# A second attention layer whose fp32 products become three single-pass products of parts, with shared arrays for the parts

## The chip, the cores and the metric

The kernel runs on one core of a Trainium2 chip. The metric is the device time of one execution in microseconds (us). The times of the kernel before are 3044.53, 3044.64 and 3044.72 us; the median is 3044.64.

The engines have short names in the profile: PE is TensorE (matmuls; PEld is its weight load), DVE is VectorE, ACT is ScalarE, POOL is GpSimd and SP is SyncE, which here issues most of the DMAs. Each engine runs its own instructions in program order; between engines there are semaphores.

## What is computed

The input is x with 2 batches, 128 channels and 64 x 64 positions, which are L = 4096 tokens per batch. Two layers follow each other:

```python
# layer 0: group norm, 4 heads of attention with rotary positions, projection, residual
x = _L0_conv_ref(x, ...)
# layer 1, on tokens t [2, 4096, 128]
t = _to_tokens(x)
t = t + _L1_attn_ref(_ln_t(t))
t = t + _L1_ffn_ref(_ln_t(t), sigma, phi, M_u, M_phi_plus, M_phi_minus, log_weights, gumbel)
x = _from_tokens(t, x)

def _L1_attn_ref(x):                       # the "second attention"
    scores = jnp.einsum('bsd,btd->bst', x, x)
    attn_weights = jax.nn.softmax(scores, axis=-1)
    return jnp.einsum('bst,btd->bsd', attn_weights, x)
```

`_ln_t` normalises each token over its 128 channels. `_L1_ffn_ref` is a spectral mixing: a causal convolution of the normalised tokens with 16 filters, then for each filter a product with a 128 x 128 matrix (`Mpp` for the plain sequence, `Mpm` for the sequence with alternating signs), and a short autoregressive part with 3 taps. The four branches on shortened sequences are weighted by a one-hot choice.

The second attention has one operand in three places: queries, keys and values are all the normalised tokens y. The scores are therefore a symmetric matrix.

## The kernel before: how the work is tiled and ordered

**Stages.** Layer 0 (`layer0`) runs attention pair by pair; beside its last pieces it is handed a generator, `beside_last()`, which normalises batch 0 for the second attention. Then `attend(0, ...)` and `attend(1, ...)` do the second attention, and a loop over convolution chunks (`chunk`, `convolve`, `mix`, `back`) does the spectral mixing.

**Second attention, L860 to L958.** The 4096 tokens are 8 blocks of 512 (NQ = 8) or 32 tiles of 128 (NT = 32). Because the scores are symmetric, only steps (j, i) with i >= j are computed, 36 per batch. A step computes the 512 x 512 block of scores as four tiles of 128 x 512 (`scores`, matmul on L877), takes exp on ACT with a fixed shift and a running sum into `den` (L886), and keeps the result as `e`, in two buffers. `turn` (L890) transposes it for steps with i > j: four transposes of 128 x 128 into one PSUM bank (L893), then a copy by ACT to SBUF that also sums (L895). `weigh` (L900) multiplies tiles of y with four tiles of `e`, or of the turned `eT`, and adds in the PSUM tile `oacc`, which has one bank for block j (summed over the whole row of steps) and one for block i (added to `oT` by DVE in each step, L930 or L932). `close` (L904) ends a row j: `fin` (L907 or L909), the reciprocal sums `rden` (L911, L912), four transposes (L915) and four updates of the tokens `tok` (L918).

The order is written out by hand in the loop at the end of `attend`: a step's scores are issued between the transposes of the step before (`late`), then the sums of the step before, and `next(beside, None)` steps a chain of side work five times in a full step. A generator that yields does one small piece each time. For batch 0 the chain is `chain(left, steps, filters, matrices)`: what layer 0 left, the normalising of batch 1 (L721 to L742), the filter tables, and the mixing's matrices. For batch 1 it is `chain(feed, second_parts)`: the convolution's input of batch 0 (`feed`, L960 to L1030) and the low parts of the matrices (L1043 to L1049).

**Matrices, L828 to L857.** For each of 16 filters, `Mpp` and `Mpm` of four branches are loaded into the tile `raw`, which has one buffer (L847, L848); DVE makes the weighted sum `pm` of four branches (`weighted_sum`, L704 once and L706 three times), writes sum and difference back into `raw` (L853, L854), casts them to the rounded type in `mx` (L855), subtracts to get the low part (L856), and SP stores this to DRAM (L857).

**Types.** A matmul of fp32 operands (F32) shows two records per product in the trace. A matmul of operands in the rounded type F32R is one pass with one record. Before, batch 1's scores, as well as the mixing (`mix`, L1166), are already written as three F32R products of a high part (the value rounded) and a low part (value minus high part). Batch 0's scores and all sums of both batches are F32.

**Statistics.** `LayerStats` (L667 to L700) takes bn_stats and bn_aggr for each of 32 token tiles on DVE (`take`), then a reciprocal root (`close`), then `normed` (L697) writes normalised tiles.

Of the kernel before, what the change touches and what calls it, by code (L numbers as in the profile page):

```python
# [44 lines left out]
WC = 4  # L45
# [18 lines left out]
def conv_attn_hybrid(ctx: ExitStack, tc: tile.TileContext, io):  # L64
# [36 lines left out]

    def group_norm(b, bank, p1, px):
# [3 lines left out]
        xn = px.tile([P, L], F32, tag="b", name=f"xn{b}")  # L106
# [57 lines left out]
    def layer0(tok, px, last, side, beside_last):  # L164


        with ExitStack() as l0:
# [222 lines left out]
            for n, (b, pr) in enumerate(units):  # L390
                if n + 1 < len(units):
                    nxt = units[n + 1]
                    if nxt[1] == 0:
                        norm = group_norm(nxt[0], bank, p1, px)
                        xn = next(norm)
                        after = prepare(*nxt, xn)
                        beside = chain(beside, norm, after[3])
                    else:
                        after = prepare(*nxt, xn)
                        beside = chain(beside, after[3])  # L400
                else:
                    beside = beside_last()
# [39 lines left out]
    def layer0_any(tok, px, last, side, beside_last):  # L442

        with ExitStack() as l0:
# [212 lines left out]
            for _ in beside_last():  # L657
                pass
# [53 lines left out]
    def layers(st, layer0):  # L712
        psum_a, right0, right1, right2 = (st.enter_context(ExitStack()) for _ in range(4))

        tok = [None, pool(right0, "tok1", side="right").tile([P, NI, C], F32, name="tok1")]
        tok[0] = pool(right1, "tok0", side="right").tile([P, NI, C], F32, name="tok0")
        last = pool(right2, "last", 2, side="right")
        px = pool(right2, "px", side="right")
        side = [None]

        def normalise(b, p, ytag, yttag):  # L721


            y = p.tile([P, NT, C], F32, tag=ytag, name=f"y{b}")
            yT = p.tile([P, L], F32R if b else F32, tag=yttag, name=f"yT{b}")

            def steps():
                stats = LayerStats(p, tok[b], f"a{b}")
                yield from stats.steps()
                for i in range(NQ):  # L730
                    for t in range(4 * i, 4 * i + 4):
                        stats.normed(y[:, t, :], t)
                    yield
                    pt = side[0](f"yT{b}_{i}")
                    for t in range(4):
                        nc.tensor.transpose(pt[:, bass.ts(t, P)], y[:, 4 * i + t, :], ident)
                    nc.vector.tensor_copy(yT[:, bass.ts(i, 512)], pt)
                    if b:
                        low = p.tile([P, 512], F32, tag="fin", name=f"low{i}")
                        nc.vector.tensor_tensor(low, pt, yT[:, bass.ts(i, 512)], ALU.subtract)  # L740
                        nc.sync.dma_start(lows_y[i], low)
                    yield  # L742

            return y, yT, steps()

        ys = [None, None]

        def beside_last():
            *ys[0], steps = normalise(0, px, "a", "b")
            yield from steps  # L750
# [8 lines left out]
        mxr = ffw.tile([P, NK, 2, C], F32R, name="mx")  # L759
        lows_y = dram.tile([NQ, P, 512], F32, name="lows_y")  # L760
        lows_m = dram.tile([NK, P, 2, C], F32, name="lows_m")
# [10 lines left out]
        pi = pool(st, "ff_in", 4)  # L772
# [55 lines left out]
        def matrices(p):  # L828
# [16 lines left out]
            for k in range(NK):  # L845
                raw = p.tile([P, NBR, 2, C], F32, tag="raw", name=f"raw{k}")
                nc.sync.dma_start(raw[:, :, 0, :], io["mpp"][:, k].rearrange("i d e -> d i e"))  # L847
                nc.sync.dma_start(raw[:, :, 1, :], io["mpm"][:, k].rearrange("i d e -> d i e"))  # L848
                yield
                pm = p.tile([P, 2, C], F32, tag="pm", name=f"pm{k}")  # L850
                weighted_sum(pm, raw, coef[:, k, :])
                own = raw[:, 0]
                nc.vector.tensor_tensor(own[:, 0, :], pm[:, 0, :], pm[:, 1, :], ALU.add)  # L853
                nc.vector.tensor_tensor(own[:, 1, :], pm[:, 0, :], pm[:, 1, :], ALU.subtract)  # L854
                nc.vector.tensor_copy(mxr[:, k], own)  # L855
                nc.vector.tensor_tensor(own, own, mxr[:, k], ALU.subtract)  # L856
                nc.sync.dma_start(lows_m[k], own)  # L857
                yield

        def attend(b, p, y, yT, oT, beside, closed=lambda j: None, lo=None):  # L860
# [6 lines left out]
            products = [(yT, yT)]  # L867
            if lo is not None:
                low = lo()
                products = [(low, yT), (yT, low), (yT, yT)]  # L870

            def scores(j, i, e, h):
                ps = psum.tile([P, 2, 512], F32, tag="st", name=f"y{b}_{j}_{i}_{h}")
                for q in range(2):
                    t = 4 * j + 2 * h + q
                    for n, (a, c) in enumerate(products):
                        nc.tensor.matmul(  # L877
                            ps[:, q, :],
                            a[:, bass.ts(t, P)],
                            c[:, bass.ts(i, 512)],  # L880
                            start=(n == 0),
                            stop=(n == len(products) - 1),
                        )
# [6 lines left out]
            def turn(j, i, e, u):  # L890
# [3 lines left out]
                eT = p.tile([P, 512], F32, tag="eT", name=f"eT{b}_{j}_{i}_{u}", bufs=5)  # L894
                nc.scalar.activation(eT, pt, AF.Copy, accum_out=den[:, 4 * i + u, j : j + 1])  # L895
                return eT

            def weigh(acc, first, es, start, stop):
                for t, e in enumerate(es):
                    nc.tensor.matmul(  # L900
                        acc, y[:, first + t, :], e, start=(start and t == 0), stop=(stop and t == len(es) - 1)
                    )
# [20 lines left out]
            def sums(j, i, e, eT, acc):  # L923
                es = [e[:, t, :] for t in range(4)]
# [15 lines left out]
            for j in range(NQ):  # L940
                acc = psum.tile([P, 2, 512], F32, tag="acc", name=f"oacc{b}_{j}", bufs=1)
                for i in range(j, NQ):
                    e = p.tile([P, 4, 512], F32, tag="e", name=f"ey{b}_{j}_{i}", bufs=2)
                    eT = []
                    for h in range(2):
# [86 lines left out]
        with ExitStack() as l1:  # L1032
            p1 = pool(l1, "l1")
            *ys[1], steps = normalise(1, p1, "y", "yT")
            fw = transform(p1)
            with ExitStack() as part:
                p = pool(part, "l1_a")
                oT = ffw.tile([P, NQ, 512], F32, tag="lo", name="oT0")
                attend(0, p1, *ys[0], oT, chain(left, steps, filters(p, fw), matrices(p)))
            right2.close()  # L1040
            mxl = ffw.tile([P, NK, 2, C], F32R, tag="lo", name="mxl")

            def second_parts():  # L1043
                for k in range(0, NK, 2):
                    low = p.tile([P, 2, 2, C], F32, tag="low", name=f"low_m{k}", bufs=1)
                    nc.sync.dma_start(low, lows_m[k : k + 2].rearrange("k p s c -> p k s c"))
                    yield
                    nc.vector.tensor_copy(mxl[:, k : k + 2], low)
                    yield  # L1049

            with ExitStack() as part:
# [3 lines left out]
                def closed(j):  # L1055
                    fed.take(range(4 * j, 4 * j + 4))
                    fed.close(range(4 * j, 4 * j + 4))

                oT = p.tile([P, NQ, 512], F32, name="oT1", bufs=1)

                def lo():
                    lo = p.tile([P, L], F32R, name="lo", bufs=1)
                    for i in range(NQ):
                        own = (p1, "fin") if i % 2 == 0 else (p, "low")
                        low = own[0].tile([P, 512], F32, tag=own[1], name=f"low_y{i}", bufs=1)
                        nc.sync.dma_start(low, lows_y[i])
                        nc.vector.tensor_copy(lo[:, bass.ts(i, 512)], low)
                    return lo

                attend(1, p1, *ys[1], oT, chain(feed(0, p, bank, fw), second_parts()), closed, lo)  # L1070
        right1.close()
# [4 lines left out]
        px = pool(st, "ff_x")  # L1076
        late_pool = pool(right1, "late", 2, side="right")

# [9 lines left out]
        def chunk(b, ro, ch, s):  # L1088
# [4 lines left out]
            for n in range(2):  # L1093
                u = f"{b}_{ro}_{ch}_{s}_{n}"
                tt = pi.tile([P, WC // 2, 2 * BP * NK], F32, tag="tt", name=f"tt{u}")
                ut = pi.tile([P, WC // 2, C], F32, tag="ut", name=f"ut{u}")
# [24 lines left out]
        xl = px.tile([P, NK * 512], F32R, name="xl", bufs=1)  # L1121
# [58 lines left out]
        def back(b, ro, oh, outs, p):  # L1180
# [7 lines left out]
            if ro == 0:  # L1188
                outs[b] = p.tile([P, L], F32, tag="out", name=f"out{b}", bufs=1)
            outr = outs[b].rearrange("p (j q r) -> p r q j", q=BP, r=2)  # L1190

            def turned(p4):
# [5 lines left out]
                v = (px if end else p).tile(  # L1198
# [41 lines left out]
        for b in range(B):  # L1240
            for ro in range(2):
                oh = (late_pool if ro else px).tile([P, L], F32, tag="oh", name=f"oh{b}_{ro}", bufs=1)
                for ch in range(NCH):
                    acc = pc.tile([P, 512], F32, tag="acc", name=f"m{b}_{ro}_{ch}")
                    for s in range(2):
                        u = f"{b}_{ro}_{ch}_{s}"
                        halves = chunk(b, ro, ch, s)
                        xh = px.tile([P, NK, WC * 4 * 2 * BP], F32R, tag="xh", name=f"xh{u}", bufs=2)
# [7 lines left out]
                if (b, ro) == (0, 0):  # L1256
                    right1.close()
                    right0.close()
                    late_pool = pool(right0, "out", 2, side="right")
# [132 lines left out]
```

## Time and profile before

| quantity | value |
|---|---|
| median of three runs | 3044.64 us |
| profiled execution | 3042.84 us |
| its span in the trace | 3041.0 us (1.84 us lie around it) |
| granted TensorE clock, mean | 0.995 |
| PE busy | 2968.3 us (98%) |
| DVE busy | 1322.6 us (43%) |
| ACT busy | 1833.4 us (60%) |
| POOL busy | 656.3 us (22%) |
| first score of batch 0, of batch 1 | 1031.56, 1452.38 us |
| first convolution matmul | 1883.2 us |

The page has six parts: busy time by engine, the span in 40 slices, the DMA queues, the chain of work that ended last, the costliest groups of instructions, and the DMA issues. In a group's row, `out<-in` are the tiles written and read, then count, busy sum in us, mean ns of one, and after the second bar the idle time of that engine just before these instructions, with who released it. Matmul records overlap, so the mean of a record is longer than the distance from one to the next. The view by windows gives the busy time of each engine in a stretch; the chain view follows the last work back to what released it.

### The profile page before, as it was taken

The page shows a single profiled execution, that of the slowest core. Times are in us where ns is not written, and L with a number is a line of the kernel's source. Part 1 is how long each engine was busy: PE and PEld are TensorE (multiplying, and loading weights), DVE is VectorE, ACT ScalarE, POOL GpSimd, SP SyncE. Part 2 cuts the span into 40 slices and gives each one's busy share as a digit, 9 for nine tenths or more (in the row PEclk, how much of TensorE's full clock was granted, in tenths as well). Part 3 has the DMA queues.
Part 4 walks back from the last instruction along what each step waited for, and adds up shares of the span by engine and source line. Part 5 has one row for each costly group of instructions (what it writes and reads, how often), then busy time and mean ns, then how long its engine had stood idle before and what let it go on. Part 6 is the DMA issues. An engine that isn't in the chain of part 4 may idle for free.

```text
span 3041.0 us, 36995 instructions
## 1 busy us (share of the span) xinstructions
PE 2968.3 (98%) x13216; PEld 1696.2 (56%) x13216; DVE 1322.6 (43%) x2236; ACT 1833.4 (60%) x2363; POOL 656.3 (22%) x1328
## 2 busy tenths in 40 slices
PE   5999999999999999999999999999999999999997
PEld 3555555555455554444555554656666666666665
DVE  5363662364332243321311113555555555555553
ACT  4999999999999734344343444444444444444442
POOL 4031120031100010000101001444444444444440
PEclk9999999999999999999999999999999999999999
DMA  4021220020000003200211000333333334333331
GB/s 145 25 82 46 63 58 6 25 81 20 6 4 6 16 25 114 70 28 4 70 35 35 10 1 16 95 88 94 92 84 80 85 73 114 80 88 81 79 81 49
DMA packets 163583, 171.52 MB, mean 56 GB/s; under 512 B 45136, under 2 KB 109408, under 8 KB 163392
## 3 DMA queue, kind: packets, MB, share of 16 engines
q1 hardware_dynamic: 119584, 131.80, 15.1%
q0 software_dynamic: 40816, 34.04, 5.1%
q10 hardware_dynamic: 2992, 3.22, 0.3%
q8 instruction: 110, 1.80, 0.3%
q14 instruction: 81, 0.66, 0.1%
HBM read 128.58 MB, written 23.40 MB: 50 GB/s over the span
## 4 chain that ended last, share of the span: by engine, by line
PE 62%; DMA 2%; DVE 2%; issue 0%; ACT 0%; SPq 0%; DVEq 0%; ACTq 0%
PE m L1166 25%; PE oacc L900 13%; PE cv L1134 9%; PE y L877 6%; PE eT L893 3%; PE ar L977 1%; PE pf L994 1%; PE bk L1216 1%; DMA raw<-in_mpm 1%; PE vt L1207 0%; DMA lows_m<-raw 0%; DVE pm L706 0%; PE o L915 0%; DMA low_y<-lows_y 0%; PE tT L972 0%; DMA low_m<-lows_m 0%
## 5 line engine op out<-in xcount | busy, mean ns | idle before, releaser
L421 ACT ACTIVATE e<-s 128x1536 f16<-128x1536 f32 (+1 forms) x704 | 936.7, 1430 | 36.4 <-PE s L178 31.5
L1143 ACT CAST xh<-cv 128x1024 fp32r<-128x1024 f32 x512 | 494.7, 1019 | 525.6 <-PE cv L1134 524.7
L1144 DVE TENSOR_TENSOR xl<-cv,xh 128x1024 fp32r<-128x1024 f32 x512 | 603.3, 1220 | 436.8 <-ACT xh L1143 346.9
L1109 POOL DMA_DIRECT2D ut<-rows x1024 | 488.4, 485 | 689.8 <-PE cv L1134 579.9
L178 PE MATMUL s<-qs,ks 128*128 128x512 f16 x2048 | 557.6, 379 | 8.5 <-ACT e L421 3.4
L178 PE MATMUL acc<-e,v 128*97 128x512 f16 x2048 | 557.3, 379 | 3.4 <-DVE accs L377 0.2
L886 ACT ACTIVATE ey<-y,nshift 128x512 f32<-128x512 f32 x288 | 195.7, 687 | 428.5 <-PE y L877 426.0
L1166 PE MATMUL m<-xh,mxl 128*128 128x512 f32 x1024 | 411.3, 402 | 0.0
L1166 PE MATMUL m<-xh,mx 128*128 128x512 f32 x1024 | 404.8, 395 | 0.0
L178 PEld LDWEIGHTS <-v 128*97 128x97 bf16 x2048 | 254.6, 124 | 214.8 <-issue 12.9
L178 PEld LDWEIGHTS <-ks 128*128 128x128 f16 x2048 | 200.6, 99 | 227.5 <-issue 42.5
L1134 PE MATMUL cv<-tt,ut 32*128 32x512 f32 x2048 | 299.4, 644 | 2.1 <-DVE xl L1144 2.1
L1166 PE MATMUL m<-xl,mx 128*128 128x512 f32 x1024 | 290.9, 416 | 0.8 <-DVE xl L1144 0.5
L1166 PEld LDWEIGHTS m<-xl,mx 128*128 128x128 f32 x1024 | 178.6, 189 | 175.0 <-issue 104.7
L900 PE MATMUL oacc<-ey,y 128*128 128x512 f32 x576 | 262.8, 592 | 0.0
L1166 PEld LDWEIGHTS m<-xh,mxl 128*128 128x128 f32 x1024 | 192.4, 188 | 91.1 <-issue 47.8
L1166 PEld LDWEIGHTS m<-xh,mx 128*128 128x128 f32 x1024 | 192.6, 188 | 43.6
L900 PE MATMUL oacc<-eT,y 128*128 128x512 f32 x448 | 206.7, 604 | 3.7 <-DVE oT L930 3.4
L877 PE MATMUL y<-yT 128*128 128x512 f32 x432 | 198.5, 531 | 1.7 <-ACT ey L886 1.7
L377 DVE COPY accs<-acc 97x512 f32<-97x512 f32 x64 | 44.2, 691 | 282.5 <-PE acc L178 282.4
L900 PEld LDWEIGHTS oacc<-ey,y 128*128 128x128 f32 x576 | 103.6, 190 | 99.3 <-issue 98.5
L900 PEld LDWEIGHTS oacc<-eT,y 128*128 128x128 f32 x448 | 80.9, 189 | 115.9 <-issue 81.6
(177 smaller groups left out, 2257.2 us busy)
## 6 DMA issues: line engine op xcount, KB each, us to landing
tt<-tables SPq DMA_DIRECT2D x1024, 64.0 KB, 3.3
tab<-in_rot SPq DMA_DIRECT2D x32, 512.0 KB, 4.2
ut<-rows POOLq DMA_DIRECT2D x1024, 16.0 KB, 3.2
qs<-term POOLq DMA_DIRECT2D x128, 64.0 KB, 2.2
rows<-uh SPq DMA_DIRECT2D x64, 128.0 KB, 1.9
ks<-term POOLq DMA_DIRECT2D x96, 64.0 KB, 1.9
accs<-back SPq DMA_DIRECT2D x32, 128.0 KB, 2.3
raw<-in_mpp SPq DMA_DIRECT2D x16, 256.0 KB, 3.0
```

The costliest lines, as they stand in the source:

```text
L178: tc.keep_in_program_order(nc.tensor.matmul(*args, **kw))
L377: nc.vector.tensor_copy(accs[:, bass.ts(half, 512)], acc[: NV * CH + 1, :])
L421: nc.scalar.activation(e[:, own, :], ps[:, own, :], AF.Exp, scale=SCORE_SCALE)
L877: nc.tensor.matmul(ps[:, q, :], a[:, bass.ts(t, P)], c[:, bass.ts(i, 512)], start=(n == 0), stop=(n == len(products) - 1),)
L886: nc.scalar.activation(e[:, 2 * h + q, :], ps[:, q, :], AF.Exp, bias=nshift, accum_out=den[:, t, i : i + 1])
L893: nc.tensor.transpose(pt[:, bass.ts(t, P)], e[:, t, bass.ts(u, P)], ident)
L900: nc.tensor.matmul(acc, y[:, first + t, :], e, start=(start and t == 0), stop=(stop and t == len(es) - 1))
L1109: nc.gpsimd.dma_start(ut[part, :, :], rows[b][ci, row : row + BP, w0 : w0 + WC // 2, :])
L1134: nc.tensor.matmul(pu[:, h, :], ut[grp, w % 2, :], tt[grp, w % 2, :], start=True, stop=True)
L1143: nc.scalar.copy(hi, pu.rearrange("d h (c k) -> d k h c", k=NK))
L1144: nc.vector.tensor_tensor(seconds[n % 2][:, :, w, 64 * g2 : 64 * g2 + 64].rearrange("d k (h c) -> d k h c", h=2), pu.rearrange("d h (c k) ...
L1166: nc.tensor.matmul(acc, m, x, start=(s == 0 and w == 0 and i == 0), stop=(s == 1 and w == WC - 1 and i == len(products) - 1),)
```

## The change

**Products.** All scores and all sums of both batches become three F32R products. The tokens' parts are `hi`, `lo` (token-major, for the sums) and `hiT`, `loT` (channel-major, for the scores). `e` is split on DVE into `ep0` (a cast) and `ep1` (e minus ep0), four tiles each per step, in `sums`. `eT` is split in `turn`: ACT copies the bank to `eT0`, DVE subtracts that from the same bank to get `eT1`.

**Arrays.** `hi`, `lo`, `hiT`, `loT` exist once. Batch 0's parts are made beside layer 0; the low parts go to DRAM (`lows`) and come back at the start of `attend(0, ...)`, a block ahead of the first row's steps (`ready`). Batch 1's parts overwrite them block by block while batch 0 is still running: `normalise` waits at `gate`, which `closed(j)` opens after row j. For that the chain of batch 0 becomes `left, filters, matrices, steps`. In batch 1, `closed(j)` loads two of the mixing's matrices and writes their high and low parts over the blocks of `hiT` and `loT` that are no longer needed; `mxr` and `mxl` are views of these two arrays. `matrices` now stores full sums to DRAM and neither casts nor subtracts.

**Convolution.** The tables and tokens of a chunk lie in two halves of fixed arrays (`tables_in` in the place of `hi`, `tokens_in`), taken in turn, where four rotating buffers were. Pools are rearranged accordingly, and some outputs take the place of `tok`.

The core of the diff:

```diff
-        def normalise(b, p, ytag, yttag):
...
+        def normalise(b, p, stage, gate=None):
+
+            stats = LayerStats(p, tok[b], f"a{b}")
+            yield from stats.steps()
+            for i in range(NQ):
+                while gate is not None and gate[0] <= i:
                     yield
+                cols = bass.ts(i, 512)
+                y = stage(i, 0)
+                for t in range(4):
+                    stats.normed(y[:, bass.ts(t, P)], 4 * i + t)
+                nc.vector.tensor_copy(hi[0][:, cols], y)
+                yield
+                pt = side[0](f"yT{b}_{i}")
+                for t in range(4):
+                    nc.tensor.transpose(pt[:, bass.ts(t, P)], y[:, bass.ts(t, P)], ident)
+                nc.vector.tensor_copy(hiT[0][:, cols], pt)
+                low = (stage(i, 1), stage(i, 0)) if b == 0 else (loT[0][:, cols], lo[0][:, cols])
+                for n, (src, first) in enumerate(((pt, hiT[0][:, cols]), (y, hi[0][:, cols]))):
+                    nc.vector.tensor_tensor(low[n], src, first, ALU.subtract)
+                    if b == 0:
+                        nc.sync.dma_start(lows[i, n], low[n])
+                yield
...
                 nc.vector.tensor_tensor(own[:, 1, :], pm[:, 0, :], pm[:, 1, :], ALU.subtract)
-                nc.vector.tensor_copy(mxr[:, k], own)
-                nc.vector.tensor_tensor(own, own, mxr[:, k], ALU.subtract)
-                nc.sync.dma_start(lows_m[k], own)
+                nc.sync.dma_start(mx[k], own)
                 yield
...
-                    for n, (a, c) in enumerate(products):
+                    for n, (a, c) in enumerate(((hiT, hiT), (hiT, loT), (loT, hiT))):
...
-                eT = p.tile([P, 512], F32, tag="eT", name=f"eT{b}_{j}_{i}_{u}", bufs=5)
-                nc.scalar.activation(eT, pt, AF.Copy, accum_out=den[:, 4 * i + u, j : j + 1])
+                eT = [p.tile([P, 512], F32R, tag=f"eT{n}", name=f"eT{n}_{b}_{j}_{i}_{u}", bufs=5) for n in range(2)]
+                nc.scalar.activation(eT[0], pt, AF.Copy, accum_out=den[:, 4 * i + u, j : j + 1])
+                nc.vector.tensor_tensor(eT[1], pt, eT[0], ALU.subtract)
...
-                for t, e in enumerate(es):
-                    nc.tensor.matmul(
-                        acc, y[:, first + t, :], e, start=(start and t == 0), stop=(stop and t == len(es) - 1)
-                    )
+                for t, (e, rest) in enumerate(es):
+                    own = bass.ts(first + t, P)
+                    for n, (a, c) in enumerate(((hi, e), (lo, e), (hi, rest))):
+                        nc.tensor.matmul(
+                            acc,
+                            a[0][:, own],
+                            c,
+                            start=(start and t == 0 and n == 0),
+                            stop=(stop and t == len(es) - 1 and n == 2),
+                        )
...
-                es = [e[:, t, :] for t in range(4)]
+                es = []
+                for t in range(4):
+                    es.append([p.tile([P, 512], F32R, tag=f"ep{n}", name=f"ep{n}_{b}_{j}_{i}_{t}", bufs=4) for n in range(2)])
+                    nc.vector.tensor_copy(es[t][0], e[:, t, :])
+                    nc.vector.tensor_tensor(es[t][1], e[:, t, :], es[t][0], ALU.subtract)
...
-                attend(0, p1, *ys[0], oT, chain(left, steps, filters(p, fw), matrices(p)))
...
+                gate = [0]
+
+                def ready(i):
+                    for n in range(2) if i == 0 else [i + 1]:
+                        if n < NQ:
+                            low = p.tile([P, 2, 512], F32, tag="low", name=f"low{n}")
+                            nc.sync.dma_start(low, lows[n].rearrange("n p c -> p n c"))
+                            nc.vector.tensor_copy(loT[0][:, bass.ts(n, 512)], low[:, 0])
+                            nc.vector.tensor_copy(lo[0][:, bass.ts(n, 512)], low[:, 1])
+
+                def closed(j):
+                    gate[0] = j + 1
...
+                steps = normalise(1, p1, stage, gate)
+                attend(0, p1, chain(left, filters(p, fw), matrices(p), steps), closed, ready)
...
                 def closed(j):
                     fed.take(range(4 * j, 4 * j + 4))
                     fed.close(range(4 * j, 4 * j + 4))
+                    own = slice(2 * j, 2 * j + 2)
+                    m = p.tile([P, 2, 2, C], F32, tag="m", name=f"m{j}")
+                    nc.sync.dma_start(m, mx[own].rearrange("k p s c -> p k s c"))
+                    nc.vector.tensor_copy(mxr[:, own], m)
+                    nc.vector.tensor_tensor(mxl[:, own], m, mxr[:, own], ALU.subtract)
+
+                attend(1, p1, feed(0, p, bank, fw), closed)
...
+        tables_in = [px.tile([P, 2, WC // 2, 2 * BP * NK], F32, tag=f"b{n}", name=f"tables_in{n}") for n in range(2)]
...
-                tt = pi.tile([P, WC // 2, 2 * BP * NK], F32, tag="tt", name=f"tt{u}")
-                ut = pi.tile([P, WC // 2, C], F32, tag="ut", name=f"ut{u}")
+                tt, ut = tables_in[n][:, turn], tokens_in[:, n, turn]
```

## The prediction

> **What bounds the kernel now.** I read three stages off the strip of the page and fixed their borders by the first score (L877) of each batch in the timeline: layer 0 to 1031.5 us, second attention of batch 0 to 1452.4, of batch 1 to 1883.2, then the convolution. The table by windows asks for exactly these; its columns are length, then the busy time of PE, PE's weight loads, DVE, ACT and POOL, then granted clock, DMA share and GB/s.
>
> ```profile
> 780.00:1031.00 251.00, 248.88 (x1168) 130.46 (x1167) 73.18 (x173) 247.54 (x187) 8.08 (x8) 1.00 0.02 6
> 1031.50:1452.40 420.90, 411.78 (x1339) 204.65 (x1337) 134.28 (x389) 168.52 (x514) 13.45 (x15) 1.00 0.15 46
> 1452.40:1883.20 430.80, 428.27 (x1572) 245.24 (x1572) 81.58 (x285) 180.71 (x538) 31.05 (x48) 1.00 0.09 26
> 1449.00:1465.00 16.00, 12.93 (x47) 9.01 (x46) 8.79 (x41) 6.04 (x17) 2.33 (x2) 0.89 0.47 138
> ```
>
> The second attention is bound by PE in both batches (411.8 of 420.9, 428.3 of 430.8 us), while DVE works 134 and 82 us of them. The end of layer 0 is bound by ACT, with DVE at 73 of 251. So work taken from PE in the second attention counts, until DVE is full.
>
> The groups by line and shape give the parts (count, busy sum, mean ns, then the idle time before them and who ended it):
>
> ```profile
> L900 PE MATMUL oacc<-ey,y 128*128 128x512 f32 x576 | 262.8, 592 | 0.0
> L900 PE MATMUL oacc<-eT,y 128*128 128x512 f32 x448 | 206.7, 604 | 3.7 <-DVE oT L930 3.4
> L877 PE MATMUL y<-yT 128*128 128x512 f32 x432 | 198.5, 531 | 1.7 <-ACT ey L886 1.7
> ...
> L895 ACT ACTIVATE eT<-eT 128x512 f32<-128x512 f32 x224 | 132.4, 604 | 13.2 <-PE eT L893 13.2
> ...
> L930 DVE TENSOR_TENSOR oT<-oacc,oT 128x512 f32<-128x512 f32 x42 | 29.0, 691 | 249.1 <-PE oacc L900 249.1
> ...
> L704 DVE TENSOR_SCALAR pm<-raw,coef 128x256 f32<-128x256 f32 x16 | 5.6, 353 | 59.7 <-DMA raw<-in_mpm 59.6
> ...
> L740 DVE TENSOR_TENSOR low<-yT,yT 128x512 f32<-128x512 f32 x8 | 5.5, 692 | 0.3
> ...
> L1067 DVE CAST lo<-low_y 128x512 fp32r<-128x512 f32 x8 | 3.4, 426 | 6.7 <-DMA low_y<-lows_y 6.7
> ```
>
> Matmul means overlap, so the pitch must come from the chain and the timeline. The chain of waits shows one fp32 sum (two records); the timeline shows the single-pass scores that batch 1 already has:
>
> ```profile
> 1199.94 3.44 PE oacc L900 x8
> ```
>
> ```profile
> 1564.87 0.39 PE L877 MATMUL y<-yT 128*128 128x512 f32 x1
> 1565.10 0.40 PE L877 MATMUL y<-yT,lo 128*128 128x512 f32 x1
> 1565.34 0.40 PE L877 MATMUL y<-lo,yT 128*128 128x512 f32 x1
> 1565.57 0.39 PE L877 MATMUL y<-yT 128*128 128x512 f32 x1
> ```
>
> Eight records in 3.44 us are four products, 0.86 us each. Single-pass products start 0.233 us apart, each with weights of its own; three are 0.70.
>
> **PE: what goes.** 0.16 us per product. Batch 0 has 144 score products in fp32 (432 records less batch 1's 144, over 2) and 256 sums (1024 records over 2 over two batches): 400 x 0.16 = 64 us. Batch 1 has its scores in three parts already: 256 x 0.16 = 41. Together **105 us**, if PE stays the bound. The Trainium skill ("FP8 and Floating Point Precision", TensorE Precision Notes) counts true FP32 as four passes; three would then cost three quarters of 0.86, and the saving would be 141. The spacing in the trace speaks against it, and I use 0.16.
>
> **DVE: what comes.** The parts are made on DVE. For each of 36 steps (j, i) per batch, four casts of e (0.426 each, nearest row L1067) and four subtractions (0.692, row L740): 4.47 us. For the 28 steps with i > j, four more subtractions that read eT's PSUM bank after ACT's copy (L895): 2.77. That is 36 x 4.47 + 28 x 2.77 = 238 us per batch. A full step after is 36 products and 16 transposes on PE, 36 x 0.233 + 1.65 (8 take about 0.80 in the timeline) = 10.05 us; DVE's part is 4.47 + 2.77 + 0.69 (oT, L930) = 7.93. The cover is PE's own 10.05, with 2 us to spare per step for all else DVE does: matrices, statistics, normalising. Per batch DVE has 134 + 238 = 372 us (less 11 for the casts and subtractions of the matrices that go) against PE's 421 - 64 = 357; in batch 1 82 + 238 + the new closing work (8 casts of m and subtractions of twice the columns, about 9) = 329 against 390. Batch 0 is no longer PE's.
>
> **The order.** Engines run in program order, so I read the compiled order of the changed kernel. In the chain of side work of batch 0, normalising batch 1 stood before filters and matrices; now it stands behind them and behind a gate. Three stretches of DVE's order follow, with the durations above, 0.336 for a normed tile, 0.278 and 0.172 for a tile's two statistics, 0.345 for tok, and 2.45 for a matrix (pm 0.353 + 3 x 0.484, sums 0.29 + 0.28, issue gaps).
>
> (For PE's side of a stretch: products x 0.233 and 0.40 for four transposes.)
>
> *Start.* The first score that needs the low part waits for a cast that stands in DVE's order behind layer 0's last copies and adds; DVE reaches it about 6.5 us after the first score. **+6.5** (0 if the scheduler's other work covers it, at most 8).
>
> *Rows j = 0, 1 and the beginning of 2.* DVE's list sums to 66 + 112.6 us, PE's to 60.5 + 103: **+15** (0 if before's own idle time of 9 us hides part of it; 30 if both engines wait in turn).
>
> *The matrices' end.* Up to matrix 10 each stands between attention work. Matrices 11 to 15 then stand back to back, and behind them all 64 statistics instructions of batch 1 and two of its normalised quarters, ahead of the eT subtractions of step (2, 3); on PE, the transposes of y1 stand ahead of that step's transposes. All matrices go through one buffer: own sums out by DMA, next matrix in by DMA. In before's timeline DVE's next pm starts 5.57 and 5.62 us after the last operation of the matrix before it; the row L704 says 59.6 us in 16 such waits. In before they cost nothing, as PE had products to go on with. Now DVE is stuck: 4.5 waits x 5.6 = 25, five matrices 12, statistics and two quarters 24.8 = 62 us. PE has some 6 us of scores left at that point: **+56**. Ends: 30, if only DVE's work and not the waits counts; 62.
>
> *Closing.* Two PSUM banks turn eT, released now by DVE's subtraction and no longer by ACT's copy (0.6 + 0.69 where 0.6 was). At row ends fin, rden and tok (0.69 + 4 x 0.345) queue behind parts of e: 8 rows x 0.5 = **+4** (0 to 16).
>
> Batch 0: -64 + 6.5 + 15 + 56 + 4 = **+18**.
>
> Batch 1 begins with 36.8 us of DVE work (last quarters of y1, 64 statistics for the feed) under 16 us of PE work plus what is left of it: **+17** (0 to 21). Row 0 has the feed too: DVE 99.6 against PE 91, **+9**. The other rows fit under PE (52 + 130 against about 255). -41 + 17 + 9 = **-15**.
>
> *The rest.* Layer 0 gets eight casts and eight subtractions of y more (9 us of DVE) and 16 stores; row one of the first fence shows their cover, ACT at 247.5 of 251: +3 for the last of them before the first score (0 to 9). Tables and tokens of the convolution now lie in arrays that the attention holds to its last weigh, so their first loads start later; a landing takes 3.3 us (tt in the issue table): +3 (-2 to 8). In the loop the loads stay two chunks ahead.
>
> Sum: 18 - 15 + 3 + 3 = +9 on the profiled execution's 3042.84 (span 3041.0 and 1.84 around it) = 3052; the median of the runs shown lies 1.8 above that, so **3054 us**.
>
> The granted clock: the window at 1449 shows 0.89 over 16 us with 3 us of PE idle, so 16 x 0.11 = 1.8 us lost per pause; it is inside the 56. The Trainium skill ("TensorE: Matmul & The Clock Gate", What's actually happening) has the clock halve after an idle window of about 3.4 us, which speaks against this change wherever DVE makes PE wait that long: six such pauses (start, matrices, three row ends, batch 1) would be 11 us, where I count one.
>
> **Rivals.**
> 1. *Cover holds but for the matrices.* PE hides start, rows 0 to 1 and batch 1's beginning (they were covered in before, with DVE at a third): 47 us fewer, about 3007. For: both engines have work in hand two steps ahead (e has two buffers). Against: DVE's sums exceed PE's in each of these stretches.
> 2. *Lockstep, slower.* Place: the full steps. PE waits for the last part of e, DVE for the next transposes. Price: one cast and subtraction (1.12) to one with ACT's copy as well (1.7) exposed in each of 56 steps, 62 to 95 us, of which 24 are counted: 3092 to 3125. It decides once side work takes more than the 2 us a step to spare, which holds in rows 0 and 1 of both batches and not behind them.
> 3. *All 105 us arrive:* about 2940 to 2985, if the matrices' stretch is not run as ordered. Speaks against it: DVE executes in order.
> 4. *The products don't get cheaper:* three at the mean record, 0.40, would be 1.2 us and 220 us lost, near 3265. The 0.233 spacing speaks against it.
>
> **How the numbers follow.** Forecast 0.45 (3038 to 3078), rival 1 0.28 (2985 to 3038), rival 2 0.18 (3078 to 3125), rival 3 0.07, rival 4 0.02. Leaving out rivals 3, 4 and the upper part of 2 gives 2985 to 3105. Within 0.2% (6 us, about what this kernel's measurement can tell from no change) lies 0.13, mostly the forecast's lower part; faster 0.35, slower 0.52.
>
> **What would show it.** PE idle some 55 us in one piece near 1230 to 1290, released by DVE's normed y1, behind waits of DVE for raw; sums at 2.8 us for twelve records; DVE near full in row 0 of both batches; batch 0 about 439 us, batch 1 about 416. If PE's idle time is spread over all steps, rival 2 is right; if the matrices do not stand in PE's way, the forecast is wrong by most of its size.

## The result, and the profile after

The changed kernel takes 2992.06 us (median of four runs, 2989.98 to 2996.01) against 3044.68 for the kernel before in the same comparison: a ratio of 0.9825, 95% interval 0.9808 to 0.9842. The forecast was 3054 us, slower; it came out 1.75% faster, inside the stated range and on its other side. The profiled execution took 2991.11 us, its span 2989.3.

By stages, from the timeline: first score of batch 0 at 1030.4 us (before 1031.6), of batch 1 at 1442.6 (1452.4), first convolution matmul at 1833.3 (1883.2). Batch 0 went from 420.8 to 412.1 us (forecast 439), batch 1 from 430.8 to 390.7 (forecast 416), the convolution from 1157.8 to 1156.0.

The changed kernel's windows of batch 0, of batch 1, and of a stretch inside batch 0 (columns as above):

```profile
1030.45:1442.57 412.12, 355.44 (x1746) 285.63 (x1745) 327.23 (x775) 171.11 (x521) 13.10 (x15) 0.92 0.16 47
1442.57:1833.30 390.73, 383.71 (x1823) 291.38 (x1821) 292.10 (x701) 180.58 (x534) 37.65 (x48) 0.99 0.09 26
```

```profile
1225.00:1255.00 30.00, 2.47 (x8) 1.37 (x8) 15.72 (x70) 0.00 (x0) 4.05 (x4) 0.50 0.24 73
1255.00:1310.00 55.00, 50.50 (x243) 40.59 (x244) 39.54 (x102) 24.87 (x76) 4.24 (x5) 0.88 0.00 1
```

Batch 1 is still bound by PE: 384 of 391 us, with DVE now at 292. Batch 0 has 57 us without a matmul, nearly all of it in one place: in the 30 us from 1225 on, PE works 2.5 us and its granted clock is 0.50. In the 55 us behind it the clock averages 0.88, so PE runs slowly for a while after it restarts.

The waits of PE in the second attention (sum in us, times, longest) name what it waited for:

```profile
PE yT L757 <- DVE lmva L693: 47.9, 2, 40.4
PE y L890 <- DVE loT L1071: 5.5, 1, 5.5
PE o L935 <- DVE fin L927: 2.4, 3, 1.0
PE oacc L916 <- DVE oT L956: 2.3, 4, 0.8
PE oacc L916 <- DVE ep L948: 1.8, 4, 0.6
```

One pause of 47.9 us in two pieces, one of 5.5 at the start, and beyond these 10 us. PE waits at the transposes of batch 1's first normalised quarter. DVE's timeline shows what keeps it, with the idle time before an instruction and its releaser in brackets:

```profile
1226.47 0.35 DVE L716 TENSOR_SCALAR pm<-raw,coef 128x256 f32<-128x256 f32 x1 [5.59 <-DMA raw<-in_mpm]
1226.86 1.53 DVE L718 SCALAR_TENSOR_TENSOR pm<-raw,coef,pm 128x256 f32<-128x256 f32 x3
1228.42 0.29 DVE L871 TENSOR_TENSOR raw<-pm 128x128 f32<-128x128 f32 x1
1228.63 0.28 DVE L872 TENSOR_TENSOR raw<-pm 128x128 f32<-128x128 f32 x1
1234.67 0.35 DVE L716 TENSOR_SCALAR pm<-raw,coef 128x256 f32<-128x256 f32 x1 [5.75 <-DMA raw<-in_mpm]
...
1242.86 0.35 DVE L716 TENSOR_SCALAR pm<-raw,coef 128x256 f32<-128x256 f32 x1 [5.74 <-DMA raw<-in_mpm]
...
1245.21 0.48 DVE L690 BATCH_NORM_STATS2 lsta<-tok 128x6 f32<-128x128 f32 x2
...
1247.93 0.34 DVE L709 TENSOR_SCALAR y<-tok,lmva,lrsa 128x128 f32<-128x128 f32 x1 [0.88 <-POOL lrsa L89]
```

The matrices come one every 8.2 us; DVE works 2.4 us on each and waits 5.6 to 5.75 for the one buffer to be stored and filled again. Statistics and y come behind the last of them. This is the stretch that the prediction described.

In the groups by shape (columns as in the section on the profile before), the last row is the matrices' wait, 26 us in all. The first row shows what the forecast expected and what did not happen: over 576 sums PE waited only 2.6 us for the parts of e, 1.8 of them for the subtractions.

```profile
L916 PE MATMUL oacc<-ep,hi 128*128 128x512 f32 x576 | 209.4, 410 | 2.7 <-DVE ep L948 1.8 <-DVE ep L947 0.8
L948 DVE TENSOR_TENSOR ep<-ey,ep 128x512 fp32r<-128x512 f32 x288 | 191.9, 683 | 5.4 <-PE oacc L916 0.4
...
L716 DVE TENSOR_SCALAR pm<-raw,coef 128x256 f32<-128x256 f32 x16 | 5.6, 348 | 26.1 <-DMA raw<-in_mpm 26.1
```

### The profile page after: what moved, and what is told of

It reads as the page before. It is cut to its first block, busy times and chain, and to the rows that moved or that the text cites. A ratio compares the mean times of both kernels' runs of the same rounds, so it can differ in the third digit from the quotient of the medians.

```text
span 2989.3 us, 40111 instructions
## 1 busy us (share of the span) xinstructions
PE 2862.9 (96%) x13872; PEld 1822.1 (61%) x13872; DVE 1738.8 (58%) x3060; ACT 1835.8 (61%) x2363; POOL 665.1 (22%) x1328
## 3 DMA queue, kind: packets, MB, share of 16 engines
q10 hardware_dynamic: 2992, 3.22, 0.3%
## 5 line engine op out<-in xcount | busy, mean ns | idle before, releaser
L1139 POOL DMA_DIRECT2D tokens_in<-rows x1024 | 490.5, 487 | 680.5 <-PE cv L1164 577.1
L1196 PE MATMUL m<-xh,loT 128*128 128x512 f32 x1024 | 409.8, 400 | 0.0
L1196 PE MATMUL m<-xh,hiT 128*128 128x512 f32 x1024 | 403.2, 394 | 0.0
L1164 PE MATMUL cv<-tables_in,tokens_in 32*128 32x512 f32 x2048 | 300.0, 645 | 1.4 <-DVE xl L1174 1.2
L1196 PE MATMUL m<-xl,hiT 128*128 128x512 f32 x1024 | 292.3, 417 | 1.2 <-DVE xl L1174 0.5
L1196 PEld LDWEIGHTS m<-xl,hiT 128*128 128x128 f32 x1024 | 178.8, 189 | 175.8 <-issue 104.7
L1196 PEld LDWEIGHTS m<-xh,loT 128*128 128x128 f32 x1024 | 192.7, 188 | 90.7 <-issue 47.8
L1196 PEld LDWEIGHTS m<-xh,hiT 128*128 128x128 f32 x1024 | 192.4, 188 | 42.2
L916 PE MATMUL oacc<-ep,hi 128*128 128x512 f32 x576 | 209.4, 410 | 2.7 <-DVE ep L948 1.8
L948 DVE TENSOR_TENSOR ep<-ey,ep 128x512 fp32r<-128x512 f32 x288 | 191.9, 683 | 5.4 <-PE oacc L916 0.4
```

What stands on the lines that cost most here:

```text
L916: nc.tensor.matmul(acc, a[0][:, own], c, start=(start and t == 0 and n == 0), stop=(stop and t == len(es) - 1 and n == 2),)
L948: nc.vector.tensor_tensor(es[t][1], e[:, t, :], es[t][0], ALU.subtract)
L1139: nc.gpsimd.dma_start(ut[part, :, :], rows[b][ci, row : row + BP, w0 : w0 + WC // 2, :])
L1164: nc.tensor.matmul(pu[:, h, :], ut[grp, w % 2, :], tt[grp, w % 2, :], start=True, stop=True)
L1196: nc.tensor.matmul(acc, m, x, start=(s == 0 and w == 0 and i == 0), stop=(s == 1 and w == WC - 1 and i == len(products) - 1),)
```

## The experiments

Two theories go through all of them. **A:** PE is the bound everywhere but in the one pause; DVE, with 12 more instructions in a full step, is covered. **B**, the prediction's: DVE is as full as PE in rows 0 to 2 and at the start of batch 1, and the pause is only where its backlog shows. For each run the second attention (first score to first convolution matmul) is measured from its trace; idle is the length less PE's busy time:

| kernel | time, us | attention | PE busy | PE idle | DVE busy |
|---|---|---|---|---|---|
| before | 3044.6 | 851.6 | 840.0 | 11.6 | 215.9 |
| changed | 2992.1 | 802.9 | 739.2 | 63.7 | 619.3 |
| e1 spread matrices | 2942.5 | 753.4 | 733.5 | 19.9 | 615.9 |
| e2 two inputs | 2951.0 | 760.0 | 737.1 | 22.9 | 615.4 |
| e3 no rest | 2971.6 | 782.1 | 738.5 | 43.6 | 326.4 |
| e4 two products | 2905.8 | 714.2 | 622.1 | 92.1 | 614.4 |
| e6 low part twice | 3037.9 | 844.2 | 776.6 | 67.6 | 787.0 |
| e7 two products, no rest | 2823.3 | 631.9 | 617.7 | 14.2 | 316.1 |
| e8 fp32 sums | 3022.5 | 833.0 | 820.6 | 12.4 | 220.1 |
| e9 half of e6 | 2973.2 | 783.5 | 749.1 | 34.4 | 700.7 |
| e10 casts by ACT | 2939.5 | 749.7 | 732.7 | 17.0 | 572.8 |

e3, e4, e6, e7, e8 and e9 are one time each; e1, e2 and e10 are medians of four. The kernel before was measured anew beside them, with medians from 3044.8 to 3047.3, so a difference of 3 us between two rows tells nothing.

**e1, the matrices spread out.**

```diff
                 nc.sync.dma_start(mx[k], own)
-                yield
+                for _ in range(3):
+                    yield
```

> Two more empty pieces after each of the 16 matrices in the chain of side work, so that a matrix comes every full step instead of every half step; all work stays. Theory A (the changed kernel, 2992 us, is bound by PE everywhere, except in one pause of 40.4 + 7.4 us with PE at half clock behind it, which comes from matrices that follow each other faster than their one buffer turns round): the pause and the slow clock behind it go, 48 to 55 us less, 2937 to 2945. Theory B (the prediction's: DVE is as full as PE in rows 0 to 2, the pause is only where its backlog shows): only the waits for DMA go, some 22 us, and the rest comes back spread over the steps, about 2970.

2942.5 us, ratio to before 0.9656 (0.9640 to 0.9672): theory A. All work is the same, and 49.5 us of attention go. The window of the attention and the longest of PE's waits in it:

```profile
1033.10:1786.50 753.40, 733.49 (x3566) 573.49 (x3564) 615.86 (x1474) 352.39 (x1052) 52.72 (x63) 0.99 0.13 40
```

```profile
PE y L891 <- DVE loT L1072: 5.3, 1, 5.3
PE oacc L917 <- DVE ep L949: 4.9, 7, 2.7
```

The wait at the transposes of y is gone. What B expected, that the rest of the wait comes back spread over the steps, did not happen: PE's idle time falls by 43.8, and its busy time by 5.7 for the same matmuls, about what the half clock behind the pause costs. Up to the eleventh matrix the two traces agree: one matrix every 10 us or so, with 12 to 17 other DVE instructions between two of them. The difference is the last five. In the changed kernel they follow each other directly, one every 8.2 us; here 9 to 27 other instructions stand between them, and DVE waits 1.6 us for the input in all, where it waited 26.1.

**e2, two inputs for the matrices.**

```diff
+            raws = p.tile([P, 2, NBR, 2, C], F32, tag="raw", name="raws")
             for k in range(NK):
-                raw = p.tile([P, NBR, 2, C], F32, tag="raw", name=f"raw{k}")
+                raw = raws[:, k % 2]
```

> The matrices' input alternates between two halves of one tile, so that the next load need not wait for the last store; order of the work unchanged. Theory A: the five matrices' waits (5.6 to 5.8 us each) shrink to what issue and landing leave, perhaps half, and the pause of 48 us falls to 20 to 35 us: 2965 to 2980. Theory B: the same 2965 to 2980 at best, or no change where PE then waits for DVE's other work. It tells how much of the pause is transfer and how much DVE's own queue.

2951.0 us, ratio 0.9689 (0.9673 to 0.9705): 41 us less, more than either theory gave it. DVE's waits for the input fell from 26.1 us to this, in the same view:

```profile
DVE pm L716 <- DMA raws<-in_mpm: 3.1, 5, 1.0
```

The expectation said that the order of the work would not change; it did. In this kernel's trace 5 to 8 other DVE instructions stand between one matrix and the next, all 16 of them, where in the changed kernel the last five follow each other directly. So the run does not separate the transfers from DVE's queue. Taken with e1 it shows what waits and bunch have in common: the matrices are asked for faster than their one buffer turns round. A second buffer (e2) or a slower asking (e1) takes both away. Why the compiled order leaves just five for the end is not shown.

**e3, no low parts of e.** In `turn` and `sums` the subtractions go, and the third product uses the high part again.

```diff
-                nc.vector.tensor_tensor(eT[1], pt, eT[0], ALU.subtract)
...
-                    nc.vector.tensor_tensor(es[t][1], e[:, t, :], es[t][0], ALU.subtract)
...
-                    for n, (a, c) in enumerate(((hi, e), (lo, e), (hi, rest))):
+                    for n, (a, c) in enumerate(((hi, e), (lo, e), (hi, e))):
```

> Leaves out the subtractions that make the low parts of e and eT; the third product of each sum uses the high part again, so PE has the same products and DVE 8 subtractions fewer per full step (4.8 us by their distance of 0.60). Theory A: DVE is covered outside the pause, so the time falls by 0 to 10 us, the pause stays: 2982 to 2992. Theory B: DVE's 24 to 41 us beyond PE's in rows 0 to 2 and at the start of batch 1 go: 2950 to 2968.

2971.6 us, 20 less, between the two. Its waits tell why: the pause is 33.1 us where it was 47.9, as the last matrix starts at 1227.3 and not at 1242.9. That is 15 of the 20. The order changed here too (three matrices follow each other directly, not five), so how much of the 15 is DVE's speed stays open. What DVE's 293 us of subtractions cost outside the pause is some 5 us; theory A in substance, though not by the number it gave.

**e4, two products a sum.** DVE still makes the low parts; nothing reads them.

```diff
-                    for n, (a, c) in enumerate(((hi, e), (lo, e), (hi, rest))):
+                    for n, (a, c) in enumerate(((hi, e), (lo, e))):
```

> Leaves out the third product of each sum (high part of the tokens by low part of e); DVE still makes the low parts. 512 products of 0.233 us fewer on PE, 119 us. Theory A: PE is the bound nearly everywhere; a full step is 8.2 us on PE against 6.7 on DVE by the distance of its instructions, so most of it arrives, 90 to 119 us less, with the rest lost in rows with side work: 2873 to 2902. Theory B (a full step costs DVE 7.9 us and 2 us of side work): less than half arrives, 2935 or more.

2905.8 us, 86 less: nearer to A. PE's busy time falls by 117 of the 119, and its idle time grows by 28, of which 13 in the pause (60.8 us: PE comes there earlier, and six matrices follow each other directly) and the rest at e, oT and fin. PE sets the pace, but DVE is not far behind it.

**e5, the first low parts cast by ACT** (on e1).

```diff
+                            cast = nc.scalar.copy if i == 0 else nc.vector.tensor_copy
-                            nc.vector.tensor_copy(loT[0][:, bass.ts(n, 512)], low[:, 0])
-                            nc.vector.tensor_copy(lo[0][:, bass.ts(n, 512)], low[:, 1])
+                            cast(loT[0][:, bass.ts(n, 512)], low[:, 0])
+                            cast(lo[0][:, bass.ts(n, 512)], low[:, 1])
```

> On the kernel with spread matrices: the first two blocks' low parts are cast by ACT, which has just ended layer 0's exp, and not by DVE, whose queue still holds layer 0's last pieces. If DVE's queue is what the second score waits for, the 5.3 us there and some of the slow clock behind it go: 4 to 7 us less than 2942.5, 2935 to 2939. If the loads themselves land late, nothing changes.

2942.2 us, no change. PE waited 5.7 us at the same place, now for ACT. The loads were not late: the one of `low` was issued at 1031.78 and landed 3.6 us later, some 3 us before the cast began at 1038.68. ACT's queue has a piece of the branch weights ahead of the cast, which waits 5.2 us for DVE; after that come 0.5 us that the profile puts down to the load of phi. So the cast moved from one queue that is held up into another. In e1, DVE's queue has ended layer 0's pieces at 1036.7, and the same branch weights hold the cast from there to 1038.8: the wait is one for the queue, as the prediction had it, but not for layer 0's pieces alone. What a cast ahead of the branch weights would gain was not measured.

**e6 and e9, DVE loaded further** (on e1). e6 issues each subtraction of e twice; e9 does that for two tiles of four.

```diff
                     nc.vector.tensor_tensor(es[t][1], e[:, t, :], es[t][0], ALU.subtract)
+                    nc.vector.tensor_tensor(es[t][1], e[:, t, :], es[t][0], ALU.subtract)
```

> On the kernel with spread matrices: every subtraction for the low part of e is issued twice (same result), 4 more on DVE per step, nothing else. Theory A counts DVE by the distance of its instructions (0.60 for this one, 6.7 us a full step, now 9.1 under PE's 10.05): only the steps with much side work show it, 5 to 30 us more than 2942.5. Theory B counts durations (0.69, 7.9 us a full step, now 10.7): each of 56 full steps grows by 0.65 us or more and side work comes on top, at least 45 us more, 2988 and up.

3037.9 us, 95 more: A's number fails, and B's is met. The changed kernel stands closer to DVE's limit than A had it. Half the dose follows:

> On the kernel with spread matrices: two of the four subtractions for the low part of e are issued twice in each step, 144 more on DVE, 86 us of its work at 0.60. Four more per step cost 95 us for 173 us of work. If DVE costs in proportion (no cover at all), 48 us more than 2942.5, about 2990. If DVE has cover up to a point and is the bound only beyond, less than a third of 95: 5 to 30 us, 2948 to 2972.

2973.2 us, 31 more, just past the 5 to 30 for cover up to a point. DVE's busy time grows by 85 us in e9 and by 171 in e6, the time by 31 and 95: the first 85 us cost 0.36 us each, the next 86 cost 0.75. There is cover, and e1 has used most of it: DVE was busy 616 of 753 us there (82%), 701 of 784 in e9 (89%), 787 of 844 in e6 (93%). Why A's number failed in e6 can be read from the table: A compared full steps without their side work, but DVE's whole work there, 787 us, is more than the 733 us that PE was busy in e1, while e9's 701 us is less.

Half of what e6 lost is not waiting. PE's idle time grew by 48 us over e1 and its busy time by 43, with the same products. The granted clock over the attention is 0.96 in e6 and 0.99 in e1; by these rounded figures (844.2 x 0.04 less 753.4 x 0.01) some 26 of the 43 us are slow clock, an estimate. The rest is not separated here; the first record behind a pause also lasts longer (0.50 us at 1318.74 below, 0.40 for the next). The timeline of PE in e6 shows one such place, and the window around it has a clock of 0.68:

```profile
1315.61 0.66 PE L757 MATMUL yT<-ident,y 128*128 128x128 f32 x4
1318.74 0.50 PE L917 MATMUL oacc<-ep,hi 128*128 128x512 f32 x1 [2.48 <-DVE ep L948]
1319.08 0.40 PE L917 MATMUL oacc<-ep,lo 128*128 128x512 f32 x1
1320.88 0.78 PE L917 MATMUL oacc<-ep,hi 128*128 128x512 f32 x2 [1.41 <-DVE ep L950]
1321.46 0.63 PE L917 MATMUL oacc<-ep,lo 128*128 128x512 f32 x1
1321.89 1.05 PE L917 MATMUL oacc<-ep,hi 128*128 128x512 f32 x2
```

```profile
1316.00:1332.00 16.00, 10.74 (x28) 6.98 (x27) 13.64 (x28) 2.79 (x8) 0.87 (x2) 0.68 0.01 2
```

At 1319 a product's record lasts 0.40 us; from 1321 on 0.63, and two together 1.05.

**e7, two products and no low parts** (on e1): the edits of e3 and e4 together.

> On the kernel with spread matrices: leaves out the third product of the sums and the subtractions that make the low parts of e and eT. 512 products fewer on PE, and DVE is out of the way. Theory A: PE alone sets the pace, 512 x 0.233 = 119 us less than 2942.5, 2820 to 2828. If ACT or the transposes' chain bound the short steps, less arrives, 2835 or more.

2823.3 us, 119.2 less, which is 512 products at 0.233. That it fits so closely is partly luck: in the profiled executions PE's busy time falls by 115.8 us (0.226 a product) and its idle time by 5.7. With DVE out of the way PE idles 14.2 of 632 us: it alone sets the pace.

**e8, one fp32 product a sum** (on e1).

```diff
+                    es.append([e[:, t, :], None])
...
-                    for n, (a, c) in enumerate(((hi, e), (lo, e), (hi, rest))):
+                    for n, (a, c) in enumerate(((hi, e),)):
                         nc.tensor.matmul(
                             acc,
-                            a[0][:, own],
+                            a[0][:, own].bitcast(F32),
```

> On the kernel with spread matrices: each sum is one fp32 product again, of e or eT with the tokens' high part seen as fp32 (leaves out the tokens' low part); no parts of e are made. 512 products of 0.86 us in place of three of 0.233. If PE sets the pace in both forms: 512 x 0.16 = 82 us more than 2942.5, 3020 to 3028. If the split form still loses time to DVE, the difference is smaller than 82.

3022.5 us, 80 more where 82 were expected. It has 293 us of subtractions and 97 of casts fewer on DVE, and its PE idles 12.4 us against 19.9 in e1: so the split form still gives back 7.5 us of idle time to DVE, and PE's busy time differs by 87.

**e10, half of the casts of e on ACT** (on e1).

```diff
-                    nc.vector.tensor_copy(es[t][0], e[:, t, :])
+                    (nc.scalar.copy if t % 2 else nc.vector.tensor_copy)(es[t][0], e[:, t, :])
```

> On the kernel with spread matrices: two of the four casts of e in each step are done by ACT in place of DVE. PE's waits for DVE in the second attention are about 12 us there. If DVE is what still costs, 5 to 10 us less: 2932 to 2938. If DVE is covered, no change (2940 to 2945); if ACT's exp and copies of eT come later for it, 2946 or more.

2939.5 us (2937.3 to 2941.5), ratio 0.9649 (0.9633 to 0.9665): 3 us below e1, with intervals that overlap. DVE gives up 43 us and ACT takes 79; PE's idle time falls by 3. By its median this is the fastest version that makes all three products.

## Why the prediction was wrong

**Right: what a product costs.** 0.16 us each over 656 products was 105 us. PE's busy time in the attention fell by 100.8, and by 106.5 once the pause is gone (e1). e7 and e8 come close to both prices separately: 0.226 us of busy time a product, and 87 us over 512 sums, 0.17 each.

**Right in mechanism, partly by luck in size: the matrices' end.** Forecast +56 for the pause. PE waits 47.9 us and loses 5.7 more by the slow clock, 53.6 together; e1 without it is 49.5 shorter. Mechanism, place and wait (5.6 us each) were as described, and waits and matrices took the 37 us counted for them. The rest of the sum came out by errors that cancel: PE had no 6 us of scores left (its last one ends at 1208.0, and DVE stands still from 1208.3), of the 24.8 us of statistics and quarters only 10.7 kept PE waiting (3.2 before its first transpose, 7.5 before the second quarter's), and the slow clock cost 5.7 where 1.8 was counted. One slip: a full step pulls the side chain four times, not five as the text above says. A matrix uses two of these, so one is asked for every half step, or 5 us, while the buffer needs 8.2.

**Wrong: DVE's sums.** The terms +15 (rows 0 and 1), +17 (batch 1's start), +9 (its row 0) and +4 (row ends) made 45 us. In the changed kernel PE's idle time outside the pause and the start is 10.3 us, and the kernel before had 11.6: as idle time these terms measured about -1. Two windows show the places, rows 0, 1 and the beginning of 2 up to the pause, and batch 1's start:

```profile
1040.00:1207.97 167.97, 166.38 (x816) 133.49 (x814) 150.94 (x336) 81.22 (x247) 0.59 (x1) 0.99 0.27 82
1442.60:1475.00 32.40, 28.23 (x116) 19.54 (x115) 29.41 (x119) 14.54 (x43) 8.09 (x8) 0.89 0.01 2
```

In the first, where +15 was forecast, PE idles 1.6 us. In the second, the place of the +17, it idles 4.2 us and the clock of 0.89 costs up to 3.6 more; the window at 1449 of the kernel before has 3.1 and 1.8 there. The step that failed is the sentence in which DVE's list "sums to 66 + 112.6 us, PE's to 60.5 + 103": it added durations. DVE's instructions overlap. The timeline of the changed kernel shows it (start, duration):

```profile
1050.52 0.68 DVE L948 TENSOR_TENSOR ep<-ey,ep 128x512 fp32r<-128x512 f32 x1
1051.12 0.76 DVE L947 CAST ep<-ey 128x512 fp32r<-128x512 f32 x2
1051.79 1.28 DVE L948 TENSOR_TENSOR ep<-ey,ep 128x512 fp32r<-128x512 f32 x2
```

A subtraction of 0.68 is followed after 0.60; two casts of 0.42 take 0.67 to the next start; two subtractions last 1.28. The trace of before had it too, at one of the matrices that I timed:

```profile
1248.53 0.68 DVE L930 TENSOR_TENSOR oT<-oacc,oT 128x512 f32<-128x512 f32 x1
1249.13 0.28 DVE L853 TENSOR_TENSOR raw<-pm 128x128 f32<-128x128 f32 x1
1249.33 0.28 DVE L854 TENSOR_TENSOR raw<-pm 128x128 f32<-128x128 f32 x1
```

0.68 and then 0.60 to the next, 0.28 and then 0.20. For PE I had taken the distance between starts and not the mean duration, and for DVE the opposite. By distance a full step costs DVE 4 x 0.34 + 9 x 0.60 = 6.8 us, not 7.9; a statistics stretch and two quarters put at 24.8 us ran from 1245.2 to 1262.8, 17.6. Measured busy time of DVE in batch 0 is 327 us (forecast 361) and in batch 1 292 (329), a tenth less in both. In rows 0 and 1 (178.6 against 163.5) and in row 0 of batch 1 (99.6 against 91) such a tenth is the whole excess over PE. At batch 1's start (36.8 against 16) it is not: DVE was nearly full there, as forecast, 29.4 of 32.4 us, but PE was busy for 28.2 of them, with more work at hand than the list had given it; why, the runs do not separate. The Trainium skill has the rule ("VectorE: DVE Perf Modes", The DRAIN you can't avoid): an instruction that is not held starts before the one ahead of it has drained. The rows above agree with it.

But the point on which it turned is narrow. The mechanism of B exists: from where e1 stands, each us of work added to DVE costs 0.36 us and then 0.75. Added to the changed kernel's 2992 (not run so), the 14% of e9 would give about 3023 and the 28% of e6 about 3087, so by this estimate a fifth more work on DVE would have made the forecast's sign right.

**Smaller terms.** Start: +6.5 forecast, 5.5 measured. Layer 0 and the convolution: +6 forecast, -2.9 measured (-1.1 and -1.8), no cost at all.

**The sum by what was measured**, in the profiled executions: products -106.5, pause +47.9, slow clock +5.7, start +5.5, other idle time -1.4, the rest -2.9: -51.7, and 3042.84 - 51.7 = 2991.1. Of the forecast's sum the products are off by 1.5, the pause with its clock by 2, DVE's sums by 46, the start and the rest by 10.

**The rivals.** Rival 1, "cover holds but for the matrices", with 0.28 and 3007 us, is what happened, but for the start, which was not hidden. The argument against it was that DVE's sums exceed PE's, the step that failed. Rival 3, that all 105 us arrive, is what e1 shows once the matrices are spread out: 2942.5 is 102 below before. Rival 2, lockstep in the full steps, did not show: 10.3 us of idle time outside pause and start, where it priced 62 to 95. e6, with its 26 waits for the second subtraction of e, shows what it would have looked like.

## What to carry to other kernels

Load an engine's queue by the distance between starts in a stretch where it runs back to back, for every engine, not by the duration in the groups; where two engines come out within a tenth of each other, that choice decides the sign. Count the side work in: e6 lost 95 us where a full step alone seemed covered. When an engine that was half idle becomes nearly full, look in the compiled order for the places where it waits for a DMA in front of work that others need: a wait that was free becomes a pause, and asking for the piece less often than its buffer turns round (here two empty pieces in a chain) gave 50 us for a line of code.

## What the runs showed of the hardware

PE's clock fell after short pauses. In the rows of e6 above, idle times of 2.48 and 1.41 us, with two products between them, are followed by products at 0.43 us distance where 0.23 is usual, from 1321 to 1331. The Trainium skill ("TensorE: Matmul & The Clock Gate", What's actually happening) puts the fall behind an idle window of about 3.4 us; no single pause here is that long. The changed kernel shows it more plainly at batch 1's start:

```profile
1459.10:1465.95 6.85, 5.14 (x20) 2.85 (x18) 6.85 (x36) 1.26 (x4) 3.14 (x4) 1.00 0.01 1
1465.95:1472.70 6.75, 6.13 (x14) 4.46 (x14) 5.65 (x18) 2.85 (x10) 1.74 (x2) 0.50 0.00 0
```

PE is busy for 5.14 of 6.85 us at full clock, no pause there lasts longer than 0.78 us, and the next 6.75 us run at half clock. So the clock can fall without one long pause; how much idle time it takes in all, these runs do not measure. In e6 PE's busy time grew by 43 us, some 26 of them by the clock, beside 48 us of waiting: there an engine that made PE stutter cost nearly twice what its waits show.
